# Turning the v rows half a slot group after they are multiplied: a graph attention layer on one core

## The chip, the cores and the metric

The kernel runs on one core of a Trainium2 chip. The metric is the device time of one execution in microseconds (us); the number that counts is the median over several executions.

## The reference

The layer has 4096 nodes of 512 features, 8 heads of 64, and a 4096 x 4096 adjacency matrix with few of its entries set (the fullest row has under forty edges). Cut to what matters:

```python
hs = layer_norm(x);  ht = layer_norm(h_target)
q = (ht @ Wq + bq) / 8;  k = hs @ Wk + bk;  v = hs @ Wv + bv        # 4096 x 512 each
logits = where(adj != 0, einsum('thd,shd->hts', q, k), -1e30)
ctx = einsum('hts,shd->thd', softmax(logits), v)
ht = layer_norm(ht + ctx @ Wo + bo)
out = layernorm(x + ht + gelu(ht @ W1) @ W2)                        # W1 512 x 2048, W2 2048 x 512
```

## The kernel before

**Sparse attention by gathered rows.** First the kernel projects all sources and writes a row of k and v for each (1024 floats, 4 KB) to `kvd` in DRAM. Beside it VectorE and ScalarE make an edge list for each target row out of the adjacency matrix. Targets are sorted by their number of edges into 32 tiles of 128 rows. A tile has a cap, the edges of its fullest row, from 11 to 39. The first sixteen tiles are of the first half of the targets (`NA` = 16), the others of the second half, whose lists are made and sorted while the first tiles are worked on.

**Slot groups.** A slot is one edge of each of a tile's 128 targets. One indirect gather on GpSimd (L987) brings one slot: for each of the 128 targets the k and v row of its edge, 512 KB. Slots are worked on in slot groups of `S` = 3; the last of a tile may have one or two. `SG` lists the 211 groups with their tile `i`, first slot `j0` and number `n`. Tiles 7 to 31 are those that the change touches.

**The ring.** Gathered slots lie in `ring`: 17 places for the first sixteen tiles, 20 for the others. `place[k]` is the first place of group k. `request(k)` issues gathers up to group `k + AHEAD`, `AHEAD` = 4. A gather can only be written into a place when all that reads the old slot there is done.

**A slot group's work** (`attention`), with a `yield` after each half:

- First half: VectorE multiplies the k parts by the tile's query (L1258) and sums over each head (L1263); ScalarE takes the exponential into `p` (L1267; L1276 for a tile's first group, written in the second half).
- Second half, for the group before: `values` multiplies its v parts by the exponentials on VectorE (L1219). The third slot's v part is multiplied on ScalarE instead (`by_scalar`, L1239 and L1242). From tile 11 on (`ADDS`) VectorE adds the second slot to the first (L1223), and from tile 21 on (`DENSE`) in every other group the third as well (L1226), so that fewer rows are left.
- Then the **turns** (L1230): for each slot left, TensorE turns four 128 x 128 blocks of the v part and adds them up in `cps` in PSUM. So a tile's context is summed and transposed at once. Two `cps` exist.
- Then `request(k)`.

**The end of a tile.** `finish` is a generator, started by the next `advance()` after `values` of the tile's last group has put it into `tails`. It masks and sums `p` (L1115, L1118), takes the reciprocal, turns it (L1131), scales the context (L1136), projects it with Wo (L1146), normalises (L697, L687 on GpSimd, L692, L1164), and turns the result into `h2T` (L1173, L1177). From tile `QUICK` = 7 on it is spread over more half groups. `p` has one buffer: a new tile's `p` can be written when the old one's readers are done. `front` makes the query of a tile ahead of time (a gather of h_target, L1026, L1030, L1033, L1040, L1045).

**The other streams.** `feed` does the feed-forward layer of a group of two tiles as soon as its `h2T` is there: `hidden` (L1367, with gelu on ScalarE, L1370) and `output` (L1376), in steps of sixteen matmuls with 256 columns or eight with 512. `end` adds the residual, normalises and stores. `other_lists` makes and sorts the second half's lists (scatters of records on GpSimd, L873). `_weave` interleaves the streams: each `yield` gives a cost, and the stream with the smallest sum goes next. What is written earlier has priority; an instruction that cannot start can be ordered behind ones written later on the same engine. Exponential and gelu need different tables on ScalarE, and a change of table is an instruction of its own.

The lines that hold turns, requests and the ring:

```python
while issued[0] <= min(k + AHEAD, len(SG) - 1):     # request(k)
    issue(issued[0])
...
if pend:                                            # second half of group k
    values(*pend.pop())
    request(k)
advance()
```

Of the kernel before, what the change touches and what calls it, by code (L numbers as in the profile page):

```python
# [17 lines left out]
P = 128  # L18
# [425 lines left out]
def adj_resnorm_kernel(  # L444
# [33 lines left out]
    nc = tc.nc  # L478
    N, D = x.shape
    F = W1.shape[1]  # L480
    H, HD = 8, 64
    KC = D // P
# [13 lines left out]
    TILES = [t for g in groups for t in g]  # L496
# [4 lines left out]
    NA, NBT = len(CAPS_A), len(CAPS_B)  # L501
# [31 lines left out]
    with tc.tile_pool(name="keep", bufs=1) as keep:  # L533
        ident = keep.tile([P, P], F32, name="ident")
# [16 lines left out]
        with ExitStack() as late:  # L551
# [20 lines left out]
            turns = {"wide": 0, "signs": 0}  # L572
# [311 lines left out]
            def project(order, t=None):  # L884
# [73 lines left out]
                with tc.manual_schedule(engines={mybir.EngineType.DVE}):  # L958
                    request(0, t)
                    measure(0)  # L960
                    scale(0)
                    turn(0)
                    request(1)
                    measure(1)
                    scale(1)
                for n in range(2, 4):
                    request(n)
# [86 lines left out]
            if short:  # L1054
                SG[:-(-TILES[0][1] // S)] = [(0, 0, short)] + [(0, j0, S) for j0 in
                                                              range(short, TILES[0][1], S)]
            kvs, rests, fronts = {}, {}, {}
            place = [11]
            for i, _, n in SG:
                if place[-1] + n > RING[i >= NA]:  # L1060
# [4 lines left out]
            issued = [0]  # L1065

            def step(gens, i):

                if i in gens and next(gens[i], StopIteration) is StopIteration:
                    del gens[i]  # L1070

            def request(k):


                while issued[0] <= min(k + AHEAD, len(SG) - 1):
                    issue(issued[0])
                    mine = set(range(place[issued[0]], place[issued[0]] + SG[issued[0]][2]))
                    for m in range(k, issued[0]):
                        assert not mine & set(range(place[m], place[m] + SG[m][2]))
                    issued[0] += 1  # L1080

# [7 lines left out]
            def issue(k):  # L1089

                for d in (1, 2):
                    if k + d < len(SG) and SG[k + d][1] == 0 and SG[k + d][0] - 3 in turned:
                        begin(SG[k + d][0], d)
                i, j0, n = SG[k]
                if j0 == 0:
                    prefetch(i + 1)
                    prefetch(i + 2)
                    begin(i, 0)
                    if TILES[i][1] > RE:
                        rests[i] = rest_of(i)  # L1100
                        next(rests[i])
                elif j0 + n > 12 and i in rests:
                    for _ in rests.pop(i):
                        pass
                kvs[k] = ring[:, place[k]:place[k] + n, :]
                for j in range(n):
                    gather(kvs[k][:, j, :], kvd[0:N + 1, :], recs[i][:, E0 + j0 + j:E0 + j0 + j + 1])
# [73 lines left out]
            def go_on():  # L1181
                for i in list(fronts):
                    step(fronts, i)
# [18 lines left out]
            def attention():  # L1202


                tails, pend = [], []

                def advance():
                    go_on()
                    for t in list(tails):
                        if next(t, StopIteration) is StopIteration:  # L1210
                            tails.remove(t)

                def values(i, j0, n, kv, p, cps, after):

                    m = n - 1 if n == S else n
                    v4 = kv[:, :m, D:].rearrange("p j (h d) -> p j h d", h=H)
                    nc.vector.tensor_tensor(v4, v4, p[:, j0:j0 + m, :].unsqueeze(3)  # L1219
                                            .to_broadcast([P, m, H, HD]), ALU.mult)  # L1220
                    slots = list(range(n))
                    if m > 1 and i >= ADDS and TILES[i][1] < HEAVY:
                        nc.vector.tensor_add(kv[:, 0, D:], kv[:, 0, D:], kv[:, 1, D:])  # L1223
                        slots.remove(1)
                        if n == S and i >= DENSE and j0 // S % 2:
                            nc.vector.tensor_add(kv[:, 0, D:], kv[:, 0, D:], kv[:, S - 1, D:])  # L1226
                            slots.remove(S - 1)
                    for j in slots:
                        for c in range(KC):
                            nc.tensor.matmul(cps[:, c, :], kv[:, j, D + c * P:D + (c + 1) * P], ident,  # L1230
                                             is_transpose=True, start=j0 + j == 0 and c == 0,
                                             stop=j0 + n == TILES[i][1] and j == slots[-1],
                                             skip_group_check=True)
                    if after is not None:
                        tails.append(after)

                def by_scalar(kv, lg):
                    pa = sp.tile([P, H], F32, name="pa")
                    nc.scalar.activation(pa, lg[:, S - 1, :], AF.Exp)  # L1239
                    for hd in range(H):  # L1240
                        v = kv[:, S - 1, D + hd * HD:D + (hd + 1) * HD]
                        newest[:] = [nc.scalar.mul(v, v, pa[:, hd:hd + 1]).ins]  # L1242

                request(0)
                yield 0.0
                k = 0
                for group in GROUPS:
                    hs = []
                    mv = sp.tile([P, 2, 2], F32, name="mv2")
                    cost = 0.5 * UNIT * len(group) / 2 / sum(TILES[i][1] for i in group)  # L1250
                    for i in group:
                        cps = ps.tile([P, KC, P], F32, name="cps", bufs=2)
                        while k < len(SG) and SG[k][0] == i:
                            _, j0, n = SG[k]
                            while i not in tqs:
                                step(fronts, i)
                            kv, tq = kvs.pop(k), tqs[i]
                            nc.vector.tensor_tensor(kv[:, :n, :D], kv[:, :n, :D],  # L1258
                                                    tq[:, :D].unsqueeze(1).to_broadcast([P, n, D]),
                                                    ALU.mult)  # L1260
                            lg = sp.tile([P, S, H], F32, name="lg")
                            latest[:] = [lg[:, 0, 0:1]]
                            logits[:] = [nc.vector.tensor_reduce(  # L1263
                                lg[:, :n, :], kv[:, :n, :D].rearrange("p j (h d) -> p j h d", h=H),
                                AX.X, ALU.add).ins]
                            if j0 > 0:
                                nc.scalar.activation(p[:, j0:j0 + n, :], lg[:, :n, :], AF.Exp)  # L1267
                            advance()
                            yield cost * n
                            if pend:  # L1270
                                values(*pend.pop())
                                request(k)
                            advance()
                            if j0 == 0:
                                p = sp.tile([P, MAXE, H], F32, name="p", bufs=1)
                                nc.scalar.activation(p[:, :n, :], lg[:, :n, :], AF.Exp)  # L1276
                            if n == S:
                                by_scalar(kv, lg)
                            last = j0 + n == TILES[i][1]
                            after = finish(i, p, cps, group, hs, mv) if last else None  # L1280
                            pend.append((i, j0, n, kv, p, cps, after))
                            yield cost * n
                            k += 1
                values(*pend.pop())
                while tails:
                    advance()
                    yield 3.0
                verdict()
# [139 lines left out]
            QUICK = 7  # L1428
# [45 lines left out]
            def fill():  # L1474
# [4 lines left out]
                for cost in _take(ed, FILL * steps):  # L1479
                    yield cost  # L1480

            att = attention()
            _weave((projections(), 0), (prepare(), 0), (fill(), 0))
            src.close()
# [59 lines left out]
```

## Time and profile before

| What | us |
|---|---|
| median of 3 runs | 1792.74 (1791.04 to 1794.76) |
| profiled execution, its own time | 1786.53 |
| its span, first to last instruction | 1784.8 |
| PE, matmuls, busy | 1663.4 |
| DVE (VectorE) busy | 1422.9 |
| ACT (ScalarE) busy | 1236.9 |
| POOL (GpSimd) busy | 1005.6 |
| gathers of k and v rows, L987, 603 of 1303 ns | 785.6 |
| turns, L1230, 1828 of 280 ns (overlapping) | 245.6 |

PE is TensorE's matmuls and PEld its weight loads, which overlap. A row of waits reads: who waited, the tile and line it was to work on, after the arrow the engine, tile and line that it waited for, then us in total, times, and the longest. In a timeline a row is start, length, engine, line, operation, tiles, shapes, number merged, and in brackets the idle time before it with what ended it. "issue" is idle time in which the engine waited for nothing that the profile shows. The stages by the profile: up to 285 us projections and the first lists; from there attention of the tiles with the feed-forward layer woven in; from about 1680 the feed-forward layer of the last tiles alone.

### The profile page before, as it was taken

The numbers are of one execution on the slowest core, as the hardware profiler recorded it, in microseconds if no ns is written. First come the engines' busy times: TensorE is split into PE (matmuls) and PEld (weight loads), VectorE is DVE, ScalarE is ACT, GpSimd is POOL, SyncE is SP. The second block draws the span as 40 slices with busy tenths as digits, with TensorE's granted clock in tenths as the row PEclk, the third lists the DMA queues.
The fourth block names the chain that finished last, engine by engine and source line by source line (L and its number), as shares of the span: only waits on it lengthen the run. The fifth ranks groups of instructions, "written<-read, shape, count | busy, mean of one in ns | idle before, by whom it ended". The sixth has DMA issues, their size and how long they took to land. (4 is left out here: it accounts for less than half of the span.)

```text
span 1784.8 us, 22466 instructions
## 1 busy us (share of the span) xinstructions
PE 1663.4 (93%) x6850; PEld 1074.3 (60%) x6850; DVE 1422.9 (80%) x2447; ACT 1236.9 (69%) x3131; POOL 1005.6 (56%) x822
## 2 busy tenths in 40 slices
PE   7989994889999999898888999999999999999997
PEld 3434443656666766665555766666666666656665
DVE  6888787879688989897878888989888888987500
ACT  5776663667777878676667877787878777876511
POOL 1000156765556666677777688866686766665101
PEclk9999997899999999999999999999999999999999
DMA  9999988978778798767777798987777867665000
GB/s 350 362 391 367 360 269 304 336 242 282 268 256 299 272 316 277 248 205 252 243 273 272 244 316 286 304 278 237 246 257 247 298 218 255 233 230 189 20 5 26
DMA packets 141610, 461.00 MB, mean 258 GB/s; under 512 B 18036, under 2 KB 23048, under 8 KB 141480
## 3 DMA queue, kind: packets, MB, share of 16 engines
q0 software_dynamic: 96272, 342.33, 56.6%
q1 hardware_dynamic: 37392, 94.06, 14.8%
q10 hardware_dynamic: 7816, 23.08, 3.3%
q8 instruction: 57, 0.93, 0.2%
q14 instruction: 73, 0.60, 0.1%
HBM read 430.61 MB, written 28.79 MB: 257 GB/s over the span
## 5 line engine op out<-in xcount | busy, mean ns | idle before, releaser
L987 POOL DMA_INDIRECT kv<-kvd,rec x603 | 785.6, 1303 | 342.2 <-issue 117.4
L1367 PE MATMUL pf<-h2T,w 128*128 128x256 f32 (+1 forms) x2176 | 473.7, 371 | 3.4 <-ACT h2T L1177 3.4
L1376 PE MATMUL po<-w,gt 128*128 128x512 f32 x1024 | 465.4, 596 | 2.7 <-ACT gt L1370 2.7
L1367 PEld LDWEIGHTS pf<-h2T,w 128*128 128x128 f32 x2176 | 391.1, 193 | 72.5 <-issue 22.2
L1258 DVE TENSOR_TENSOR kv<-kv,tq 128x1536 f32<-128x1536 f32 (+2 forms) x211 | 351.9, 1677 | 66.7 <-DMA kv<-kvd,rec 54.0
L1242 ACT ACTIVATE kv<-kv,pa 128x64 f32<-128x64 f32 x1520 | 390.7, 336 | 4.4
L1263 DVE TENSOR_REDUCE lg<-kv 128x24 f32<-128x1536 f32 (+2 forms) x211 | 350.4, 1667 | 0.3
L1376 PEld LDWEIGHTS po<-w,gt 128*128 128x128 f32 x1024 | 188.2, 191 | 196.8 <-issue 192.8
L1230 PE MATMUL cps<-ident,kv 128*128 128x128 f32 x1828 | 245.6, 280 | 51.9 <-DVE kv L1219 34.1
L1230 PEld LDWEIGHTS cps<-ident,kv 128*128 128x128 f32 x1828 | 216.7, 144 | 127.6 <-DVE kv L1219 40.6
L1219 DVE TENSOR_TENSOR kv<-kv,p 128x1024 f32<-128x1024 f32 (+1 forms) x211 | 251.2, 1192 | 25.2 <-ACT p L1267 23.7
L687 POOL TENSOR_TENSOR n_rs<-n_ve,mhalf 128x2 f32<-128x2 f32 (+2 forms) x51 | 53.5, 1049 | 338.7 <-DVE n_ve L680 155.1
L735 ACT ACTIVATE kv<-kv 128x1024 uint8<-128x1024 int32 x128 | 134.5, 1053 | 60.1 <-DMA kv<-in_adj_dram 24.3
L1370 ACT ACT_TABLE_LOAD x109 | 139.8, 1283 | 1.8
L1370 ACT ACTIVATE gt<-pf 128x512 f32<-128x512 f32 x128 | 76.4, 597 | 88.2 <-PE pf L1367 84.9
L1146 PE MATMUL t<-wo,rb 128*128 128x512 f32 x256 | 120.0, 610 | 7.9 <-DVE rb L1136 7.9
L949 PE MATMUL pq<-wk,h2T 128*128 128x512 f32 x256 | 118.8, 607 | 4.2 <-DMA wk<-in_L_gnn_Wk_dram 2.9
L949 PE MATMUL pq<-wv,h2T 128*128 128x512 f32 x256 | 117.3, 601 | 4.2 <-DVE rbc L662 2.9
L1040 PE MATMUL t<-wq,tq 128*128 128x512 f32 x256 | 115.4, 593 | 2.4 <-ACT tq L1033 2.4
L744 DVE MAX8 cand<-kv 128x8 uint16<-128x171 uint16 (+1 forms) x384 | 108.0, 324 | 1.2
L1267 ACT ACTIVATE p<-lg 128x24 f32<-128x24 f32 (+2 forms) x179 | 39.0, 218 | 100.3 <-DVE lg L1263 99.4
L1267 ACT ACT_TABLE_LOAD x71 | 91.1, 1283 | 1.2
(164 smaller groups left out, 1534.6 us busy)
## 6 DMA issues: line engine op xcount, KB each, us to landing
kv<-in_adj_dram SPq DMA_DIRECT2D x128, 512.0 KB, 6.8
kvd<-tq ACTq DMA_DIRECT2D x23, 512.0 KB, 7.0
kv<-kvd,rec POOLq DMA_INDIRECT x603, 5.9
kv<-in_L_gnn_h_target_dram SPq DMA_DIRECT2D x32, 256.0 KB, 7.2
kv<-in_x_dram SPq DMA_DIRECT2D x15, 512.0 KB, 8.3
kvd<-kv ACTq DMA_DIRECT2D x9, 512.0 KB, 7.0
w<-in_L_gnn_W_dram SPq DMA_DIRECT2D x4, 1024.0 KB, 7.2
w<-in_L_gnn_W_dram ACTq DMA_DIRECT2D x4, 1024.0 KB, 15.4
```

Source lines behind the costliest of these rows:

```text
L735: nc.scalar.activation(sg, a, AF.Sign, accum_out=dpart[:, i, h:h + 1])
L949: nc.tensor.matmul(pkv, hT[:, kc, j * P:(j + 1) * P], w[:, kc, :], start=kc == 0, stop=kc == KC - 1)
L987: issues[:] = [nc.gpsimd.indirect_dma_start(out=dst, out_offset=None, in_=table[:, :], in_offset=bass.IndirectOffsetOnAxis(ap=idx, axis=0) ...
L1219: nc.vector.tensor_tensor(v4, v4, p[:, j0:j0 + m, :].unsqueeze(3) .to_broadcast([P, m, H, HD]), ALU.mult)
L1230: nc.tensor.matmul(cps[:, c, :], kv[:, j, D + c * P:D + (c + 1) * P], ident, is_transpose=True, start=j0 + j == 0 and c == 0, stop=j0 + n ...
L1242: newest[:] = [nc.scalar.mul(v, v, pa[:, hd:hd + 1]).ins]
L1258: nc.vector.tensor_tensor(kv[:, :n, :D], kv[:, :n, :D], tq[:, :D].unsqueeze(1).to_broadcast([P, n, D]), ALU.mult)
L1263: logits[:] = [nc.vector.tensor_reduce(lg[:, :n, :], kv[:, :n, :D].rearrange("p j (h d) -> p j h d", h=H), AX.X, ALU.add).ins]
L1267: nc.scalar.activation(p[:, j0:j0 + n, :], lg[:, :n, :], AF.Exp)
L1367: nc.tensor.matmul(pf[:, k, :], w1[(f0 + k) // KC][:, kc, (f0 + k) % KC * P:((f0 + k) % KC + 1) * P], h2T[:, kc, :w], start=kc == 0, stop= ...
L1370: nc.scalar.activation(gt, pf, AF.Gelu_apprx_tanh)
L1376: nc.tensor.matmul(po[j], gt[:, k, j * P:(j + 1) * P], w2[(f0 + k) // KC][:, (f0 + k) % KC, :], start=False, stop=f0 + k == FC - 1, skip_g ...
```

## The change

`values` no longer issues the turns. It wraps them, and the appending of `finish`, in a function `turn`, which is kept in `turns`. `add_up` issues what is kept. It is called in the first half of the next group, after the exponential, and followed by `request(k - 1)`. For tiles before `QUICK` = 7 it is also called right after `values`, so that these tiles keep their order. The request in the second half stays for tiles before 7 and after 16; from tile 7 to 16, where the ring has no room for a sixth group, only the later request is left. `held_up` tells the assertion in `request` that a group's places are in use until its turns are issued. At the end of the last tile `add_up` is called at once.

```diff
                     mine = set(range(place[issued[0]], place[issued[0]] + SG[issued[0]][2]))
-                    for m in range(k, issued[0]):
+                    for m in range(max(k - len(held_up), 0), issued[0]):
                         assert not mine & set(range(place[m], place[m] + SG[m][2]))
...
-                    for j in slots:
-                        for c in range(KC):
-                            nc.tensor.matmul(cps[:, c, :], kv[:, j, D + c * P:D + (c + 1) * P], ident,
-                                             is_transpose=True, start=j0 + j == 0 and c == 0,
-                                             stop=j0 + n == TILES[i][1] and j == slots[-1],
-                                             skip_group_check=True)
-                    if after is not None:
-                        tails.append(after)
+
+                    def turn():
+                        for j in slots:
+                            for c in range(KC):
+                                nc.tensor.matmul(cps[:, c, :], kv[:, j, D + c * P:D + (c + 1) * P],
+                                                 ident, is_transpose=True,
+                                                 start=j0 + j == 0 and c == 0,
+                                                 stop=j0 + n == TILES[i][1] and j == slots[-1],
+                                                 skip_group_check=True)
+                        if after is not None:
+                            tails.append(after)
+
+                    turns.append(turn)
+                    held_up[:] = turns
+
+                def add_up():
+                    while turns:
+                        turns.pop(0)()
+                    held_up.clear()
...
                             if j0 > 0:
                                 nc.scalar.activation(p[:, j0:j0 + n, :], lg[:, :n, :], AF.Exp)
+                            add_up()
+                            if k > 0:
+                                request(k - 1)
                             advance()
                             yield cost * n
                             if pend:
                                 values(*pend.pop())
-                                request(k)
+                                if i < QUICK:
+                                    add_up()
+                                if i < QUICK or i > NA:
+                                    request(k)
                             advance()
...
                 values(*pend.pop())
+                add_up()
                 while tails:
                     advance()
```

More of the change, by code (lines that the diff above doesn't have):

```diff
@@ L1056, in adj_resnorm_kernel @@
                                                               range(short, TILES[0][1], S)]
-            kvs, rests, fronts = {}, {}, {}
+            kvs, rests, fronts, held_up = {}, {}, {}, []
             place = [11]
@@ L1202, in attention @@
             def attention():
-                tails, pend = [], []
+                tails, pend, turns = [], [], []
                 def advance():
```

## The prediction

> **What bounds the kernel now.** I read the table of engines, the slices, the waits of PE, a table of stretches, and last the timeline of PE at its longest wait.
>
> ```profile
> PE 1663.4 (93%) x6850; PEld 1074.3 (60%) x6850; DVE 1422.9 (80%) x2447; ACT 1236.9 (69%) x3131; POOL 1005.6 (56%) x822
> PE   7989994889999999898888999999999999999997
> PEclk9999997899999999999999999999999999999999
> ```
> PE is busy for 93% of the span, and from the twenty-third slice on it hardly pauses. Below 9 it falls in slices 7 to 9 (the start of the first tiles, which the change leaves alone) and in 17 and 19 to 22. Matmuls overlap in these records, so I checked the distance between starts: 0.43 us for 512 columns, 0.215 for 256 and 0.109 for a turn, back to back. A busy PE is a full PE here, and only its waits can be won.
>
> ```profile
> PE cps L1230 <- DVE kv L1223: 15.7, 10, 7.1
> PE cps L1230 <- DVE kv L1219: 9.7, 4, 7.1
> PE t L1030 <- DVE kv L854: 5.8, 1, 5.8
> PE t L1173 <- ACT h L1164: 5.7, 4, 4.2
> PE pf L1367 <- ACT h2T L1177: 3.2, 3, 2.7
> PE po L1376 <- ACT gt L1370: 2.7, 1, 2.7
> PE cps L1230 <- DVE kv L1226: 1.4, 2, 0.8
> ```
> These are PE's waits from 544 us, where the eighth tile's first exponential (L1276) runs, to the end: us in total, times, longest. The turns (L1230) wait 15.7 + 9.7 + 1.4 = 26.8 us for VectorE to finish the rows they are to turn. That is all the change can take away directly, 1.5% of the time. By slots it is three places: 7.13 at 833, 7.09 at 934, and 6.65 in four pieces from 873 to 893; 3.0 more at 779, 947 and 971; the rest is in pieces under 0.9.
>
> ```profile
> 544.00:721.00 177.00, 174.26 (x802) 121.84 (x801) 156.97 (x274) 146.23 (x371) 114.60 (x91) 0.99 0.82 282
> 779.00:980.00 201.00, 173.27 (x770) 121.17 (x771) 165.77 (x180) 140.24 (x388) 159.06 (x123) 0.95 0.76 254
> 1035.00:1384.00 349.00, 340.47 (x1478) 227.22 (x1477) 312.03 (x339) 273.19 (x739) 257.93 (x201) 1.00 0.81 270
> 1384.00:1680.00 296.00, 292.07 (x1197) 191.72 (x1197) 251.12 (x330) 218.81 (x558) 173.53 (x139) 0.99 0.64 214
> ```
> The columns are length, then PE, PEld, DVE, ACT and POOL busy, clock, DMA share and GB/s. Outside 779 to 980 PE has about 98% of each stretch. Inside it PE is idle for 28 us, and the fullest engine is POOL: 159 us busy, and 123 instructions with some 0.3 us between them, 37 us more: 196 of 201. The row of POOL's gathers in that stretch:
>
> ```profile
> L987 POOL DMA_INDIRECT kv<-kvd,rec x92 | 121.5, 1321 | 31.2 <-issue 17.9 <-DMA rec<-rec 3.8 <-DMA kv<-kvd,rec 3.0
> ```
> Its releasers (the last columns) name no turn: gathers wait there for their queue alone. So POOL sets the pace of the rows there; VectorE waits for gathers (6.4 us at 816, 8.9 at 922) and PE for VectorE:
>
> ```profile
> 822.61 3.60 PE L1376 MATMUL po<-w,gt 128*128 128x512 f32 x8
> 833.33 1.97 PE L1230 MATMUL cps<-ident,kv 128*128 128x128 f32 x8 [7.13 <-DVE kv L1223]
> 835.09 1.06 PE L1131 MATMUL t<-ident,rb 128*128 128x128 f32 x4
> 835.95 4.64 PE L1367 MATMUL pf<-h2T,w 128*128 128x256 f32 x16
> ```
> Feed-forward work that could have run (L1367, 16 matmuls) stands behind the waiting turns.
>
> **What the Trainium skill says.** "TensorE: Matmul & The Clock Gate", section "Step-by-step: what each phase is for": matmuls stay in program order, only weight loads are pulled ahead. The rows above agree: L1367 starts after the turns. Section "What's actually happening" of that page: after an idle window of about 3.4 us the array runs at half clock. Agrees: behind the 7.13 us wait, eight turns took 1.97 us (1.04 elsewhere), the next four transposes 1.06 (0.60), sixteen 256-column matmuls 4.64 (3.62): 2.4 us lost after the wait; behind the 7.09 us wait twelve turns took 2.82 for 1.47. "DMA: Bandwidth & Descriptors", section "SWDGE vs HWDGE vs iDMA": of the software queues one is allocated. The profile has one, q0, with 56.6% of the DMA time; all gathers share it.
>
> **The change part by part.** No instruction is added or removed; every row, turn and gather stays, in another order.
>
> *Turns of tiles 7 to 31 move half a slot group back.* 169 slot groups from tile 7's start (544.1 us) to the last tile's (1641.5) make 6.5 us a group, so half of one is 3.25 us. That is also about one feed unit (sixteen 256-column or eight 512-column matmuls, 16 x 0.215 = 8 x 0.43 = 3.4 us), which now stands ahead of the turns. Above: each wait shrinks by up to 3.25 on its own: 3 x 3.25 + 3.0 + about 2.9 (small ones) = 15.7. Below: where POOL fixes when rows come, PE's total wait is the largest lead that it ever has over the rows, and 3.25 us more room takes off 3.25 once, not at each wait. In 779 to 980 POOL is full at 196 of 201, so I take the lower way there: 3.4 (one unit). Outside it the small waits go: 2.9. Two waits over 3.4 us become shorter, one perhaps falls under the window: I count 1.5 of the 2.4 and 1.35 us of slow clock. Sum: **7.8 us gained**, bounds 3 and 18.
>
> *Gathers of tiles 7 to 16 are requested half a slot group later*, behind the turns that free their places; each such request is three instructions on POOL's queue (L987, 1.31 us each, 5.9 to landing), and first ones of a tile bring SP's or POOL's record load and a gather of h_target with them. From tile 17 on requests keep their place, but can meet turns that come later. What hides it: turns lag their v rows by 11.2 us (median) in tiles 7 to 10, 6.7 in 11 and 12, and 5 to 6.6 later, so rows 3.25 us later are mostly still ahead of PE; between 779 and 980 gathers wait for no turn. If the cover is gone, that is the second rival. I take 0, bounds 0 and 20. Queued behind a gather that waits are scatters of records (L873, 16 of them), the powers (L687) and the output stores (L1340); for these wait the second half's lists and the ends of groups, both not due soon.
>
> *A tile's finish starts half a slot group later*, and so do its transposes, projection and h2T. Only the feed of that group waits for it. In steady state it is one shift of 3.25 us; PE waits for h2T for 3.2 us in three places, and the last tile's finish is emitted at once, so the end of the program (96 us of feed alone from 1680 to 1776) is not moved. I take 0, bounds -1 and 4.
>
> *A wait is added at each tile's start.* `p` has one buffer. Before, the old tile's masking and sum (L1115, L1118) were written ahead of the new tile's first exponential (L1276), with half a slot group before the rows need it; now they are written after it, and the exponentials of two groups must wait for them. 0.3 us (L1115) + 0.42 (L1118) + 0.22 (L1276), and a table load of 1.28 us ahead of 19 of 32 (mean 0.76): 1.7 us in which VectorE can lack the next v multiplication. Behind the waiting exponential on ACT are by_scalar's eight multiplications and gelu. 25 tiles x 1.7 = 42 us of VectorE, which has 37 us idle of 349 in tiles 17 to 24; PE's lag covers 1.7 us except where it is nearly 0. In tiles 13 to 30, 35 of 128 slot groups have a lag under 3.25 us, 11 of the 29 in tiles 13 to 15. I charge the three starts in tiles 13 to 15 by that share, 3 x 1.7 x 11/29 = 2 us; bounds 0 and 12 (35/128 of the 42).
>
> Sum: -7.8 + 0 + 0 + 2 = about **-6 us**. The profiled execution took 1786.5 us (span 1784.8 and 1.7 around it), 6.2 under the median of the runs shown, 1792.74. The waits are its waits; the difference is carried to the median: 1792.7 - 6 = 1786.7.
>
> **The rivals.** *Each wait shrinks on its own.* If POOL's pace is not fixed but eases between its three late places, 15.7 and most of the slow clock go, less 2: -16, 1777. For it: between these places the lag recovers to 8 to 12 us. Against it: POOL's 196 of 201.
>
> *The ring becomes the bound (slower).* In tiles 7 to 15 some five slot groups share seventeen places; a place is free only after its turns. Five groups take 33 us; a round of gathers (5 us with gaps), landing (5.9), product and reduction (3.4, and 3.4 of the next group), v multiplication and addition (1.9) and turns (1.4) is 21, plus queueing. Later turns and later requests add 3.25 to the round. Over some 70 groups, 14 rounds, that is 45 us if there were no slack. POOL already waits 38.1 us for turns from 544 to 1010, 32 times. It decides from the point where a gather's landing plus product comes later than PE's lag can hide: if a third of the rounds have no slack, 15 us are lost, against 7.8 won and 2 paid: +9, 1802. Against it: in tiles 7 to 10, where the waits for turns are, the lag is longest.
>
> *Little changes.* If the order of PE's queue follows readiness and not the place in the text (an instruction can be ordered past one that is not ready: VectorE has a one-slot product at 448 ahead of three full ones of its tile), then turns behind ready feed work stand where they stood: about -1, 1792.
>
> **How the numbers follow.** My forecast (-6) has 0.38, waits that shrink one by one 0.16, the ring and other new waits 0.28, little change 0.18. A measurement of this kernel can tell about 0.2%, 3.6 us, from no change. From the forecast case 0.31 is faster by more than that and 0.07 within; from the second case all is faster; little change gives 0.03 faster, 0.13 within and 0.02 slower; the ring gives 0.28 slower. Sum: faster 0.50, same 0.20, slower 0.30. The likeliest case has its own range, 1780 to 1791; eight in ten need 1774 (most of the second case) to 1804 (most of the ring case).
>
> **What would show it.** Right: PE's waits at L1230's place for VectorE after 544 us fall from 26.8 to about 20, and one feed unit stands between v multiplication and turn. The ring case would show POOL's waits for turns above 38 us up to 1010 and VectorE's waits for kv gathers above 47 us (35.7 and 11.7 before). The p wait would show as VectorE waiting for L1276 or the first L1267 of a tile, by over 20 us more than now (19.8). The forecast is wrong if PE's total of waits after 544 us rises, or if PE idles at other lines by as much as it wins at the turns.

## The result, and the profile after

| | median, us | runs | ratio to before |
|---|---|---|---|
| before | 1793.82 (1786.53 to 1810.01) | 22 | |
| changed | 1789.62 (1778.38 to 1791.79) | 22 | 0.9959, 95% 0.9943 to 0.9975 |

The ratio, taken over all runs, is 0.41% below 1, 7 us of 1794; the two medians alone lie 4.2 us apart; the forecast was -6. That agreement is the trap of this case. The two profiled executions stand the other way round: 1786.53 us before, 1791.79 after. Up to the first exponential of tile 7 (L1276 before, L1293 after), a part that the change leaves alone, they need 544.1 and 550.4 us; from there to PE's end 1229.0 and 1228.2. So the traces show no gain where the change acts. They still show what became of each step.

The table of engines and two of the slices, after:

```profile
PE 1667.9 (93%) x6850; PEld 1078.8 (60%) x6850; DVE 1422.1 (79%) x2447; ACT 1233.5 (69%) x3127; POOL 1037.1 (58%) x822
PE   7999986789999999988888999999999999999997
PEclk9999997898999999999998999999999999999998
```
PE dips in about the same slices as before. POOL is busy for 31 us more, 20.6 of them in the 603 gathers (806.2 against 785.6 at L987).

PE's waits from 544 us to the end, after (total, times, longest):

```profile
PE t L1173 <- ACT h L1164: 12.9, 5, 6.8
PE cps L1232 <- DVE kv L1219: 8.6, 4, 7.0
PE cps L1232 <- DVE kv L1223: 8.5, 8, 2.8
PE t L1131 <- ACT rb L1125: 7.9, 1, 7.9
PE cps L1232 <- DVE lg L1274: 2.5, 1, 2.5
PE pf L1385 <- ACT h2T L1177: 2.3, 4, 1.7
```
The turns (now L1232) wait 8.6 + 8.5 + 2.5 = 19.6 us for VectorE where they waited 26.8: as forecast. But `finish` now waits too: 12.9 us at L1173 (5.7 before) and 7.9 at L1131. By kind, with every releaser counted, the turns fell from 27.5 to 20.0, finish rose from 8.2 to 22.9, the query of the next tile fell from 7.9 to 2.7 and the feed from 6.0 to 3.2. PE's idle time after tile 7's start went from 49.5 to 48.9 us.

PE's timeline of the changed kernel at two of the three places at which it stopped before, 833 and 934 us:

```profile
822.43 3.60 PE L1394 MATMUL po<-w,gt 128*128 128x512 f32 x8
825.86 1.03 PE L1385 MATMUL pf<-h2T,w 128*128 128x256 f32 x4
834.76 1.12 PE L1131 MATMUL t<-ident,rb 128*128 128x128 f32 x4 [7.87 <-ACT rb L1125]
835.66 3.98 PE L1385 MATMUL pf<-h2T,w 128*128 128x256 f32 x10
...
932.34 3.60 PE L1394 MATMUL po<-w,gt 128*128 128x512 f32 x8
942.89 2.82 PE L1232 MATMUL cps<-ident,kv 128*128 128x128 f32 x12 [6.95 <-DVE kv L1219]
945.50 1.06 PE L1131 MATMUL t<-ident,rb 128*128 128x128 f32 x4
```
The stop at 834 is the old one at 833 (7.13 us) under another name: the transposes of the reciprocal (L1131) now come first, and the turns come later. 26.8 less that 7.13 is 19.7: the fall at the turns is a renaming. The stop at 943 is the old one at 934 (7.09), with its name and nearly its length. Twelve turns behind it took 2.82 us as before (1.47 elsewhere): the half clock after an idle window, which "TensorE: Matmul & The Clock Gate", section "What's actually happening", of the Trainium skill describes, was not escaped.

Why the turns' new room doesn't help is in VectorE's timeline at the same two places:

```profile
829.03 1.76 DVE L1269 TENSOR_TENSOR kv<-kv,tq 128x1536 f32<-128x1536 f32 x1 [2.49 <-issue]
830.71 0.17 DVE L1121 TENSOR_SCALAR ri<-sums 128x8 f32<-128x8 f32 x1
832.18 1.76 DVE L1269 TENSOR_TENSOR kv<-kv,tq 128x1536 f32<-128x1536 f32 x1 [1.31 <-DMA kv<-kvd,rec]
833.86 0.20 DVE L1122 RECIPROCAL ri<-ri 128x8 f32<-128x8 f32 x1
...
939.80 1.76 DVE L1269 TENSOR_TENSOR kv<-kv,tq 128x1536 f32<-128x1536 f32 x1 [4.27 <-issue]
941.48 0.15 DVE L794 TENSOR_TENSOR bad<-num,rec 128x1 f32<-128x1 f32 x1
941.54 0.17 DVE L1121 TENSOR_SCALAR ri<-sums 128x8 f32<-128x8 f32 x1
941.62 1.22 DVE L1219 TENSOR_TENSOR kv<-kv,p 128x1024 f32<-128x1024 f32 x1
```
The small steps of `finish` and the v multiplication stand in VectorE's queue behind k products (L1269) of later slot groups that started late. For the one at 832.18 the profile names the gather that it waited for; for the other two it names nothing ("issue"), but the trace has the landings: the last rows of a gather came in at 828.95 and at 939.72 us, 0.08 us before each of them started. Whatever PE needs from VectorE next, be it a reciprocal or v rows, comes after that product.

The stretch of the three stops (length; PE, PEld, DVE, ACT, POOL busy; clock, DMA share, GB/s), after:

```profile
779.00:980.00 201.00, 175.94 (x763) 121.73 (x763) 167.59 (x184) 142.29 (x394) 159.93 (x122) 0.94 0.78 255
```
POOL is as full as before (159.93 and 122 gaps of 0.3 us: 197 of 201) and PE idles for 25 us (28 before).

### The profile page after: what moved, and what is told of

The parts are those of the page before. It is cut to its first block, busy times and chain, and to the rows that moved or that the text cites. A ratio compares the mean times of both kernels' runs of the same rounds, so it can differ in the third digit from the quotient of the medians.

```text
span 1790.1 us, 22456 instructions
## 1 busy us (share of the span) xinstructions
PE 1667.9 (93%) x6850; PEld 1078.8 (60%) x6850; DVE 1422.1 (79%) x2447; ACT 1233.5 (69%) x3127; POOL 1037.1 (58%) x822
## 3 DMA queue, kind: packets, MB, share of 16 engines
q0 software_dynamic: 96272, 342.33, 56.6%
q1 hardware_dynamic: 37392, 94.06, 14.7%
## 5 line engine op out<-in xcount | busy, mean ns | idle before, releaser
L987 POOL DMA_INDIRECT kv<-kvd,rec x603 | 806.2, 1337 | 314.3 <-issue 127.5
L1269 DVE TENSOR_TENSOR kv<-kv,tq 128x1536 f32<-128x1536 f32 (+2 forms) x211 | 352.4, 1678 | 64.9 <-DMA kv<-kvd,rec 54.5
L1232 PEld LDWEIGHTS cps<-ident,kv 128*128 128x128 f32 x1828 | 218.0, 145 | 112.5 <-issue 40.9
L1232 PE MATMUL cps<-ident,kv 128*128 128x128 f32 x1828 | 245.6, 281 | 41.9 <-DVE kv L1219 30.5
L687 POOL TENSOR_TENSOR n_rs<-n_ve,mhalf 128x2 f32<-128x2 f32 (+2 forms) x51 | 48.2, 946 | 330.4 <-DVE n_ve L680 108.2
L949 PE MATMUL pq<-wv,h2T 128*128 128x512 f32 x256 | 121.8, 621 | 10.6 <-ACT kv L735 4.4
L949 PEld LDWEIGHTS pq<-wv,h2T 128*128 128x128 f32 x256 | 50.5, 199 | 77.1 <-issue 61.9
```

What stands on the lines that cost most here:

```text
L949: nc.tensor.matmul(pkv, hT[:, kc, j * P:(j + 1) * P], w[:, kc, :], start=kc == 0, stop=kc == KC - 1)
L987: issues[:] = [nc.gpsimd.indirect_dma_start(out=dst, out_offset=None, in_=table[:, :], in_offset=bass.IndirectOffsetOnAxis(ap=idx, axis=0) ...
L1269: nc.vector.tensor_tensor(kv[:, :n, :D], kv[:, :n, :D], tq[:, :D].unsqueeze(1).to_broadcast([P, n, D]), ALU.mult)
```

## The experiments

The theories: *room counts once* (the forecast), *waits shrink one by one*, *the ring*, and *little changes*. After the first results a fifth came up: any new order of the instructions moves the time by as much as this change does. Ratios are to runs of the kernel before on the same chip, with 95% intervals; its medians there were 1786.97, 1787.74 and 1784.83 us.

**The two kernels again.** No edit.

> The changed kernel once more, for a second profile and the gain on another set of rounds. Theory (room at the turns): ratio about 0.996 again; PE's waits for VectorE at the turns after tile 7's start near 20 us as in the first profile (26.8 before), and its waits at the finish chain (L1131, L1173) near 21 us (7.4 before): the room won at the turns is partly given back at the finish, which starts half a slot group later. Rival (the finish waits of the first profile are chance of one execution): the finish waits fall back to under 10 us in this profile while the turns stay near 20.

Measured: 1786.42 us (14 runs), 0.9987 (0.9968 to 1.0007). PE's waits from 544 us:

```profile
PE t L1173 <- ACT h L1164: 11.8, 5, 4.4
PE cps L1232 <- DVE kv L1219: 10.8, 4, 9.3
PE cps L1232 <- DVE kv L1223: 8.5, 8, 3.4
PE t L1131 <- ACT rb L1125: 8.4, 1, 8.4
```
The shift from the turns to `finish` comes back: with every releaser counted, the turns wait 19.7 us and `finish` 23.0. The gain does not: on this chip it is not told from zero.

> The kernel before once more, for a second profile: how far do PE's waits differ between two executions of the same instructions. If the waits at the turns after 544 us are again near 27 us and those at the finish chain near 7, the differences between the profiles of before and after belong to the change; if they move by 5 us or more, one profile of each can't carry them.

Measured: 1790.31 us. Tile 7 began at 547.1 us (544.1 in the other profile of the same kernel), PE idled 48.7 us from there (49.5), 23.4 of it at the turns (27.5) and 8.5 at `finish` (8.2). Two of its rows:

```profile
PE cps L1230 <- DVE kv L1223: 13.0, 5, 6.8
PE cps L1230 <- issue: 6.3, 3, 5.5
```
The turns' waits that the profile puts down to VectorE are 16.0 us in all here, and 26.8 in the other profile of the same kernel. So the fall from 26.8 to 19.6, taken alone, is no more than two executions differ by. With every releaser counted the turns wait 27.5 and 23.4 us before, 20.0 and 19.7 changed; what stands clear of the scatter is `finish`, 8.2 and 8.5 before, 22.9 and 23.0 changed. The changed kernel's two profiles differ as much ahead of tile 7: 550.4 and 547.5.

**One half of the change alone.** Turns held back in tiles 7 to 16 only, then from tile 17 on only:

```diff
-if i < QUICK:
+if i < QUICK or i > NA:
     add_up()
```

> Turns are held back only in tiles 7 to 16; from tile 17 on they follow their multiplication as before. Theory (the gain is one move of 3.4 us plus slow clock where POOL sets the pace, and 2.9 us of small waits later): about -4 us, 0.998. Rival (each wait shrinks on its own): nearly the whole gain is here, -7 us or more, 0.996 or less. Rival (ring): this half alone is slower than before, 1.002 or more, and the gain of the change is made later.

```diff
-if i < QUICK:
+if i <= NA:
     add_up()
-if i < QUICK or i > NA:
-    request(k)
+request(k)
```

> Turns are held back only from tile 17 on, where the ring has room and requests keep their place. Theory: the small waits go, -3 us, 0.998. Rival (ring hurts tiles 7 to 16): -7 us or more, better than the whole change. Rival (all of the gain is where POOL is full): no difference, 1.000.

Measured: 1787.94 (14 runs), 0.9997 (0.9980 to 1.0015), and 1787.48 (22 runs), 1.0005 (0.9989 to 1.0022). Neither half does anything that can be told (the interval of the first just reaches the 4 us that I expected of it). The three-place stage that was to pay 3.4 us lies in the first.

**Turns held back in all tiles.** The requests of the first seven tiles come half a slot group later with them.

```diff
-if i < QUICK:
-    add_up()
-if i < QUICK or i > NA:
+if i > NA:
     request(k)
```

> Turns are held back in all tiles, the first seven too, where PE waits about 24 us for VectorE at the turns in some eight places. Theory (room counts once where rows come at a pace that PE doesn't set): 3 to 6 us better than the changed kernel in the stretch of the first seven tiles, ratio 0.995. Rival (each wait shrinks on its own): 8 waits of up to 3.25 us, 15 us or more, ratio 0.990. Rival (there is too little feed work yet to stand ahead of the turns): no gain or a loss from the later finish, 0.998 to 1.003.

Measured: 1784.71 (22 runs), 0.9984 (0.9973 to 0.9995). Seven more tiles held back cost nothing, so there is no sign of a ring that fills up; they did not bring the 3 to 6 us that I expected either. From tile 7 on the text is that of the change, in another order of the instructions: there PE idles for 38.4 us (48.9 and 47.7 in the change), 26.3 of it at the turns and 6.8 at `finish`. The shift to `finish` is not in this order.

**`finish` back at its old place, the turns still late.**

```diff
+if after is not None and i >= QUICK:
+    next(after)
     turns.append(turn)
```

> As the changed kernel, but the first step of a tile's finish (mask, sum, reciprocal, L1115 to L1125) is written right after the last v multiplication again, and all its later steps half a slot group earlier; only the turns stay back. Theory (the room won at the turns is given back at the late finish): PE's waits at L1131 and L1173 after tile 7's start fall from 20 us to under 10, turns stay at about 20, and the time is 5 to 10 us under the changed kernel's: ratio 0.993 to 0.996. Rival (the finish waits are ACT and VectorE being busy and don't depend on the start): waits at L1131 and L1173 stay near 20, ratio as the changed kernel's, 0.998 to 1.000.

Measured: 1788.92 (22 runs), 1.0015 (0.9999 to 1.0032). PE's waits from 544 us:

```profile
PE cps L1232 <- DVE kv L1223: 14.7, 4, 11.5
PE cps L1232 <- DVE kv L1219: 8.8, 2, 7.2
...
PE cps L1232 <- DVE kv L1226: 3.1, 1, 3.1
PE t L1173 <- ACT h L1164: 2.8, 2, 2.6
```
`finish` is out of the way (10.6 us in all, 22.9 in the change), and the turns wait 26.8 us again. PE's idle sum is 49.5. Its timeline and VectorE's show the same stop:

```profile
824.28 0.60 PE L1131 MATMUL t<-ident,rb 128*128 128x128 f32 x4
836.38 1.97 PE L1232 MATMUL cps<-ident,kv 128*128 128x128 f32 x8 [11.50 <-DVE kv L1223]
```

```profile
826.04 1.76 DVE L1272 TENSOR_TENSOR kv<-kv,tq 128x1536 f32<-128x1536 f32 x1 [7.88 <-DMA kv<-kvd,rec]
```
The wait is kept. It falls on whichever instruction of the attention is first in PE's queue when VectorE stands before a gather that has not landed. Removing the late `finish` won nothing, since by PE's idle sum it had cost nothing.

**Late requests alone.** Turns at their old place; in tiles 7 to 16 the gathers keep the later request.

```diff
-if i < QUICK:
-    add_up()
+add_up()
```

> Turns follow their multiplication as before in all tiles; only the requests of tiles 7 to 16 come half a slot group later, as in the change. Theory (gathers there wait for POOL, not for turns): no difference, 0.999 to 1.002, VectorE's waits for kv gathers after 544 us within 10 us of the 47 before. Ring rival: slower by 5 us or more, 1.003 or more, with VectorE's waits for kv gathers over 60 us.

Measured: 1774.59 (6 runs), 0.9913 (0.9884 to 0.9941). The part of the change that I had priced at 0, with a loss of up to 20 as its other end, came out as a gain of 0.87%, 13 us by the medians. The trace is of the slowest of these six runs. VectorE's waits for gathers from 544 to 1680 us:

```profile
DVE kv L1269 <- DMA kv<-kvd,rec: 25.5, 9, 5.6
...
DVE kv L1269 <- issue: 2.1, 2, 1.1
```
That is 27.6 against 47.4 before and, in the change, this:

```profile
DVE kv L1269 <- DMA kv<-kvd,rec: 40.3, 18, 4.8
...
DVE kv L1269 <- issue: 9.4, 6, 4.3
```
The stop near 833 is gone. The stretch 790 to 840 of late requests alone:

```profile
790.00:840.00 50.00, 48.99 (x219) 32.81 (x218) 47.75 (x58) 41.16 (x111) 40.35 (x34) 1.00 0.77 249
```
and of the changed kernel:

```profile
790.00:840.00 50.00, 42.13 (x184) 29.51 (x184) 42.11 (x51) 36.25 (x98) 40.94 (x32) 0.93 0.76 241
```
POOL is equally full (40.4 and 40.9 of 50 us, with 34 and 32 gaps); it gets through its gathers earlier. From 770 to 820 us it started 23 gathers of k and v with late requests alone, 21 before and 19 in the change. Against the kernel before, two output stores come after them (from 824.6 us; the first at 814.4 before). Against the change, the gathers from 770 to 826 us were shorter (1222 ns, and 1382 in the change; 1248 before). Whether order or length is the cause was not tried.

**Is that more than another order would do?** `WAIT`, the head start that the second half's lists give to the other streams in `_weave`, is 94 cost units. At 95 or 93 the work is the same. Of PE's 6850 matmuls in order of time, set against those of the kernel before line by line, 890 and 198 stand in another place (956 in the change).

```diff
-WAIT = 94.0
+WAIT = 95.0
```

> The kernel before with the start of the second half's lists moved by one unit of the interleaving (WAIT 95 for 94): nothing of turns, requests or finish is touched, but some thousand lines of PE's order change. It measures how far the time moves by a new order alone. If it stays within 0.999 to 1.001, a ratio of 0.996 or 0.998 is the doing of the change; if it moves by 0.2% or more either way, a part of the change's 0.4% can be the order that came up by chance.

> The kernel before with WAIT 93: a second draw of an order that touches neither turns, requests nor finish. If orders scatter by 0.3%, 0.997 to 1.003; if r8 was an exception, within 0.999 to 1.001.

Measured: 1782.15 (13 runs), 0.9967 (0.9950 to 0.9983), at 95; 1779.93 (22 runs), 0.9967 (0.9953 to 0.9982), at 93. An edit that says nothing about turns or gathers is worth as much as the change. The change and late requests alone were then put into these orders:

> The whole change in the order that r8 gave (WAIT 95). Theory (the change gains some 0.3% whatever the order): 0.992 to 0.995, 0.2 to 0.4% under r8. Rival (order alone is worth 0.3% either way, and the change's gain is such a draw): 0.996 to 1.002, at or above r8's 0.9967.

> The whole change with WAIT 93, to be set against r11. Theory: 0.2 to 0.4% under r11. Rival: at r11 or above. With the pairs of WAIT 94 (0.9959 and 0.9987), 95 and 93 this makes three draws of the change's effect.

> Late requests alone (turns as before), in the order that r8 gave (WAIT 95). r6 had 0.9913 in the old order and r8 alone 0.9967. Theory (late requests gain by themselves: POOL stands less behind gathers that wait for turns): 0.988 to 0.992, some 0.5 to 0.8% under r8. Rival (r6 was an order that came up by chance): 0.995 to 1.000, not below r8.

Measured: the change at 95: 1790.32 (22 runs), 1.0034 (1.0021 to 1.0048); at 93: 1768.63 (6 runs), 0.9917 (0.9884 to 0.9950); late requests alone at 95: 1773.80 (11 runs), 0.9943 (0.9924 to 0.9962). Each divided by the kernel before in the same order, with the two half-widths added in squares (at 93 both ratios come from one chip; at 95 they come from two, each taken against the kernel at 94 there):

| `WAIT` | change / before | late requests / before |
|---|---|---|
| 94 | 0.9959 ± 0.0016, again 0.9987 ± 0.0020 | 0.9913 ± 0.0029 |
| 95 | 1.0034 / 0.9967 = 1.0067 ± 0.0021 | 0.9943 / 0.9967 = 0.9976 ± 0.0025 |
| 93 | 0.9917 / 0.9967 = 0.9950 ± 0.0036 | not tried |

The change is faster in two orders and slower in the third, each time beyond its interval (the second measurement at 94 not). PE's longest waits at 95 (from 530 us on), first of the kernel before and then of the change:

```profile
PE cps L1230 <- DVE kv L1223: 17.7, 4, 11.8
```

```profile
PE t L1131 <- ACT rb L1125: 10.5, 1, 10.5
PE t L1173 <- ACT h L1164: 8.5, 5, 5.5
```
and at 93, in the same way:

```profile
PE cps L1230 <- DVE kv L1223: 14.0, 9, 4.7
```

```profile
PE cps L1232 <- DVE kv L1223: 18.4, 7, 10.6
PE t L1173 <- ACT h L1164: 6.9, 2, 6.6
```
The stop near 830 is in all four. At 95 the change makes it shorter (11.8 to 10.5) and the kernel slower; at 93 it makes it longer (4.7 to 10.6) and the kernel faster. So this stop does not decide the time. Nor is the shift from the turns to `finish` in every order: at 95 the turns wait 16.8 us (26.7 before) and `finish` 23.2 (12.2), but at 93 the turns wait 25.7 (24.5) and `finish` 6.9 (7.4). Late requests alone at 95 still have the stop near 830, with 6.7 us, and VectorE's waits for gathers are not clearly shorter there: 38.7 us, or 45.2 with one wait that the profile puts down to a scatter of records, against 45.7 in the kernel before. By idle time, PE stands still after tile 7's start for 56.7 us at 95 and 41.5 at 93, against 47.0 and 44.2 of the kernel before in these orders. At 94 it was 48.9 and 47.7 changed, 49.5 and 48.7 before. The mean of the three orders (the two profiles of 94 averaged first) is 48.8 changed and 46.8 before, within orders that range from 41.5 to 56.7: no sign that PE waits less.

## Why the prediction was right or wrong

The number held: 1789.6 in 1774 to 1804, on the side that had half of the chance. The reason given for it did not, and that the sum came so near is luck: in two other orders the same change measured +0.67% and -0.50%. By its own steps:

- **"Turns move back: 7.8 us gained."** The sign it named came (26.8 to 19.6 at the turns), though a second profile of the kernel before has 16.0 in its place; the gain behind it did not. The failed step is "3.25 us more room takes off 3.25 once": the stop at 833 went to L1131 and grew from 7.13 to 7.87, the one at 934 stayed at 6.95, and of the 6.65 us in pieces around 880 some 5.7 remained. The 1.5 us of slow clock did not come back either. The room itself was mis-sized: the median lag of a turn behind its v multiplication is 11.3 us in tiles 7 to 10 (11.2 before), 3.7 in 11 and 12 (6.7), 7.4 in 17 to 24 (5.5) and 8.7 in 25 to 30 (6.4). It grew by about 2 us, not 3.25, and only where PE hardly waits. From tile 11 on most turns need VectorE's additions too, which this lag leaves out, in the prediction as here; behind the last VectorE work that a turn needs, the lag is 1.5 us in 11 and 12 (4.9 before), 4.6 in 17 to 24 (4.0) and 5.3 in 25 to 30 (3.9). Where the room was wanted, PE soon stood at the next thing that it needed from the same VectorE queue.
- **"Finish half a slot group later: 0."** In this order `finish` was not off the path: its waits rose by 14.7 us. The sum was still right, for a reason that I had not seen: these were the waits that the turns had lost (the experiment with `finish` early).
- **"Gathers half a slot group later: 0, at worst 20 lost."** Wrong side. Alone this part gained 0.87% in one order, and in another 0.24%, which is not told from zero. I had looked only at rows that come later, and not at what else is in POOL's queue and gets ahead or stays behind. In the whole change the gain does not appear: VectorE's waits for gathers are 49.7 us (47.4 before), with the unnamed waits of its k products counted in.
- **"A wait at each tile's start: +2."** The exponential (L1293) waits for the sum (L1118) three times, 3.9 us in all; VectorE's waits at the v multiplication fell from 19.8 to 6.1 us. That fall belongs to this order (10.7 before and 12.7 changed at 95, 14.7 and 15.1 at 93), but in none of them is there a loss near the 20 us that would have shown this cost. ScalarE's timeline shows one of the three:

```profile
826.58 0.22 ACT L1293 ACTIVATE p<-lg 128x24 f32<-128x24 f32 x1 [2.47 <-DVE sums L1118]
```
- **The ring** fell: POOL's waits for turns up to 1010 us went down, from 38.1 to 32.3, and holding back seven more tiles was no loss. In 779 to 980, where hardly any gather had waited for turns, they rose from 2.1 to 5.8.
- **Waits that shrink one by one** fell with the two long stops that didn't shrink.
- **Little changes** gave the right account of PE's sum (-0.6 us), but not by its mechanism, since the order did change.
- **What would make it wrong** was named: that PE idles at other lines by as much as it wins at the turns. That is what both pairs of profiles show.
- **Two readings were off.** The 56.6% of queue q0 is its share of the sixteen engines' whole span; of the DMA time it is three quarters. And POOL is "full" at 196 of 201 in part because of a few long gathers: the median one takes 0.95 us there, and 22 of the 92 over 1.5 us make up 51 of the 121.5 us (26 of 92 in the change, 16 of 96 with late requests alone). What lengthens those, POOL's own work or the transfers behind it, was not tried, so that POOL itself sets the pace is argued and not shown.

What the 0.41% is made of stays open. It is as large as the effect of an order that means nothing (0.33% twice; the changed kernel at 95 and at 93, on one chip, differs by 1.2%), and over three orders the effect of the change has no settled sign. The working had no term for that: a change of order draws a new one, and here the draw is worth about as much as the effect that I was pricing. The two fastest versions were late requests alone (0.9913) and the change with `WAIT` at 93 (0.9917), each on six runs; how much of each is such a draw was not settled.

## What to carry to other kernels

When an instruction that waits is moved back, look up what then stands first in its engine's queue and whether that waits for the same producer; compare the sum of the waits, and not the row that was to shrink. Follow such a stop to the engine in front of it, and that one's to the one before: here from PE over VectorE's k product to POOL's queue of gathers, where half a slot group of delay did more than at the end of the chain in one order, and nothing that could be told in another. And before a gain of a few tenths of a per cent is credited to a reordering, measure an order that means nothing.

## What was not expected of the hardware

Two executions of the same program differ by 3 us up to the same instruction at 545 us (544.1 and 547.1; 550.4 and 547.5), so a pair of profiles cannot carry a difference of 6. Of equal indirect gathers on POOL's queue, 92 in 779 to 980 us took 1336 ns in the changed kernel, 96 took 1231 with late requests alone, and 92 took 1321 before; single ones of the changed kernel lie between 0.94 and 3.70 us.

The length of a wait alone does not tell whether the half clock follows. Below are eight turns of the kernel before behind the same wait of 3.48 us in its two profiles, at full clock in the first and at half in the second; and eight turns of the changed kernel at half clock behind 2.80 us, less than the 3.4 us that the prediction counted with.

```profile
880.52 1.09 PE L1230 MATMUL cps<-ident,kv 128*128 128x128 f32 x8 [3.48 <-DVE kv L1223]
884.93 1.97 PE L1230 MATMUL cps<-ident,kv 128*128 128x128 f32 x8 [3.48 <-DVE kv L1223]
873.22 1.97 PE L1232 MATMUL cps<-ident,kv 128*128 128x128 f32 x8 [2.80 <-DVE kv L1223]
```
